# Another order of the key copies, the experts' loads and the experts' sums in a transformer block with two attentions and routed experts

## The chip, the cores and the metric

The kernel runs on one core of a Trainium2 chip. The time is the device time of one execution in microseconds; of several executions the median is given.

## The reference

The input is 32 sequences of 256 tokens of 128 numbers, all float32. With `xn = layernorm(x)` the output is `x + attention(xn) + ffn(xn)`:

- `attention`: 16 heads of 8 numbers; the keys attended to are the 256 tokens of the same sequence. A score is the covariance of a query and a key plus the product of their variances, over 8. Softmax over keys, sum of values, projection by Wo.
- `ffn`: a second block over the same tokens, in which the roles of sequence and batch are exchanged. Layernorm, a causal attention over the 32 "sequences" at one token place, projection, residual `x1`; then a second layernorm, a router over 8 experts, and for each token the two best experts: `gelu(h w1[e]) w2[e]`, weighted by the router's gate, summed and added to `x1`.

```
probs = softmax(cov(q, k) / D + var(q) var(k) / D)
x1 = xn + causal_attention(layernorm(xn)) @ out_proj
hn2 = layernorm(x1)
gates, top2 = top_k(softmax(hn2 @ router_w.T), 2)
out = x + probs @ v @ Wo + x1 + sum over top2 of gate * gelu(hn2 @ w1[e]) @ w2[e]
```

## The kernel before

The order in which each engine works is written out by hand: the instructions of an engine run in the order of the program's lines, and engines wait for each other by semaphores only.

**Causal attention** (`first_rounds`, `last_rounds`, L450 to L538). 16 chunks of 512 tokens go through layernorm, projections, scores, weights and the router's logits. `resd` in device memory gets `x + x1` (L427), `zx` in SBUF keeps the normalised tokens for the experts, `lg` the logits.

**The other attention** (`step`, L926). 32 sequences with two groups of eight heads give NU = 64 units. A unit has eight heads and is walked through in four steps, t = 8u + 0, 2, 4, 6, called x = 0, 2, 4, 6 below; each step first does two heads of scores in two senses (`scores_of`, L597): `sm`, query against key, LEAD = 14 heads ahead, for the maximum over keys (VectorE, L625); and `sT`, key against query, for the exponentials (ScalarE, L628). The maximum is turned and added to the queries "qa" two units later (L674), so that the exponentials need no more subtraction. Around these, by x:

- x = 0: in odd units `turn` (transposes of a finished sequence, L682, copied at L684), in even ones `close` (projection L690, added to the residual at L691); then `weigh_head` for the last unit's second half (pav, L637).
- x = 2: `project` and `project_rest` for a sequence two ahead (L560, ScalarE's sq L566 and qk L568, VectorE's L577 and L579).
- x = 4: `divide_lessen` (transposes L656, L659, division L664, L667, the maximum's addition L674), `turn_qk` for unit u + 3 (transposes L587 into a PSUM bank "pqk", and three copies out of it: qa by ScalarE L592, the keys "ka" in two halves, each masked for one of two heads, by VectorE L594 and ScalarE L595), and in even units `gather` (GpSimd, L551: copies one sequence's tokens out of `xnT` into "xs", two buffers) and `fetch_residual` (SyncE, L555).
- x = 6: `weigh_head` for this unit's first half.

PSUM has eight banks: four go round among sT, pav, pt, px and pe (`bank_u`), four among sm, pp, pqk, po, py and ph (`bank_w`). A new tile waits until every reader of the fourth last one is done.

**Routing** (`route`, L720) is a generator. `some(n)` (L919) lets it go n items on before each step: in units 0 to 11 four items a unit, which are VectorE's small operations over all tokens; from unit 12 on eight a unit, which are GpSimd's 128 indirect DMAs (L804) that scatter rows of `zx` to their place in `xsd`, sorted by expert.

**Experts** (`experts`, L864). At t = 256, the start of unit 32, 71 blocks of 256 rows are done in one go. `fetch` (L824) loads a block's rows from `xsd` by a DMA on GpSimd's queue, four blocks ahead; `select` (L828) reads the block's expert into a VectorE register and copies its weights; `enter` (L834) transposes the rows and scales them (L840); `hidden` (L844) is the first layer with Gelu (L850); `leave` (L852) the second layer, the copy "ye" (L861) and the store to `ysd`, also on GpSimd's queue (L862).

**Sums** (`combine`, L887), a second generator, is then drawn on by five items a unit. For each sequence, four indirect DMAs on GpSimd's queue gather its tokens' two expert rows (L894); two sequences later GpSimd multiplies by the gates (L907) and adds twice to the residual (L909). If the residual isn't loaded yet, an item does nothing. `part` (L881) stores a sequence (SyncE, L885) once both `close` and the sums have been added.

Of the kernel before, what the change touches and what calls it, by code (L numbers as in the profile page):

```python
# [11 lines left out]
F32 = mybir.dt.float32  # L12
BF16 = mybir.dt.bfloat16
I32 = mybir.dt.int32
AF = mybir.ActivationFunctionType
# [4 lines left out]
P = 128  # L20
NB = 32
SEQ = 256
NH, HD = 16, 8
NE, FF = 8, 256
NCHUNK = 16
NTILE = 64
BLK = 256
NBLK = 2 * NTILE * P // BLK + NE - 1
# [40 lines left out]
def block_kernel(  # L69
# [21 lines left out]
    nc = tc.nc  # L91
# [9 lines left out]
    half = cst[:, C_HALF:C_HALF + 2]  # L101
# [11 lines left out]
    xsd = dp.tile([NBLK * BLK, P], F32, name="xsd")  # L113
# [37 lines left out]
    def bank_u(shape, name):  # L151
        return pu.tile(shape, F32, tag="u", name=name)

    def bank_w(shape, name):
        return pw.tile(shape, F32, tag="w", name=name)
# [389 lines left out]
    NU = 2 * NB  # L545
# [7 lines left out]
    def fetch_residual(s):  # L553
        res[s] = b2.tile([P, 2, P], F32, tag="res", name=f"res{s}", bufs=NB // 2 + 4)
        nc.sync.dma_start(res[s], resd[s].rearrange("(i t) e -> t i e", t=P))  # L555
# [25 lines left out]
    def turn_qk(u):  # L581

        s, g = divmod(u, 2)
        pp = bank_w([P, 2, 2, P], f"pqk{u}")
        for n in range(2):
            for ti in range(2):
                nc.tensor.transpose(  # L587
                    pp[:, n, ti, :], qkts[s % NQ][:, ti, n, g].rearrange("p m r -> p (m r)"), ident
                )
        pp = pp.rearrange("p n t m -> p n (t m)")  # L590
        qas[u] = qa = bh.tile([P, SEQ], F32, tag="qa", name=f"qa{u}", bufs=4)
        nc.scalar.copy(qa, pp[:, 0, :])  # L592
        kas[u] = ka = bh.tile([P, 2, SEQ], F32, tag="ka", name=f"ka{u}", bufs=4)
        nc.vector.tensor_scalar(ka[:, 0, :], pp[:, 1, :], half[:, 0:1], None, ALU.mult)  # L594
        nc.scalar.activation(ka[:, 1, :], pp[:, 1, :], AF.Identity, scale=half[:, 1:2])  # L595

    def scores_of(t):  # L597

# [31 lines left out]
    def weigh_head(u, h):  # L630

        s, g = divmod(u, 2)
        if h == 0:
            pos[u] = bank_u([P, SEQ], f"pav{u}")
        for ti in range(2):
            for j in range(4):
                nc.tensor.matmul(  # L637
                    pos[u][32 * j:32 * j + 32, :],
                    vaugs[s % NV][:, ti, 4 * j + 2 * g + h, :],
                    exs[8 * u + 4 * h + j][:, ti, :],  # L640
                    start=(h == 0 and ti == 0),
                    stop=(h == 1 and ti == 1),
                )
        if h == 1:
            oas[u] = b2.tile([P, SEQ], F32, tag="oa", name=f"oa{u}")
            nc.scalar.copy(oas[u], pos.pop(u))
# [31 lines left out]
    def turn(s):  # L678
        pt = bank_w([P, 2, P], f"po{s}")
        o = ot.pop(s)  # L680
        for si in range(2):
            nc.tensor.transpose(pt[:, si, :], o[:, si, :], ident)  # L682
        oT = b2.tile([P, SEQ], F32, tag="oT", name=f"boT{s}")
        nc.vector.tensor_copy(oT, pt.rearrange("p i s -> p (i s)"))  # L684
        return oT

    def close(s, oT):
        py = bank_w([P, 2, P], f"py{s}")
        for i in range(2):
            nc.tensor.matmul(py[:, i, :], oT[:, i * P:(i + 1) * P], wo, start=True, stop=True)  # L690
        nc.vector.tensor_tensor(res[s], res[s], py, ALU.add)  # L691
        part(s)
# [120 lines left out]
    xb, wb, hb, yb = {}, {}, {}, {}  # L813
# [8 lines left out]
        gt["wall"] = wall  # L822

    def fetch(n):  # L824
        xb[n] = c2.tile([P, 2, P], F32, tag="xb", name=f"xb{n}", bufs=5)
        nc.gpsimd.dma_start(xb[n], xsd[n * BLK:(n + 1) * BLK].rearrange("(p j) w -> p j w", j=2))  # L826

    def select(n):  # L828
        e = nc.vector.value_load(gt["ebi"][0:1, n, :], min_val=0, max_val=NE - 1)
        w = c2.tile([P, 2, FF], F32, tag="w", name=f"w{n}", bufs=3)  # L830
        nc.vector.tensor_copy(w, gt["wall"][:, bass.ds(e, 1)].rearrange("p o t f -> p (o t) f"))
        wb[n] = w[:, 0, :], w[:, 1, :].rearrange("p (f h) -> p f h", f=2)

    def enter(n):  # L834
        px = bank_u([P, 2, P], f"px{n}")
        for j in range(2):
            nc.tensor.transpose(px[:, j, :], xb[n][:, j, :], ident)  # L837
        del xb[n]
        hb[n] = c2.tile([P, BLK], F32, tag="xT", name=f"xT{n}")
        nc.scalar.activation(  # L840
            hb[n], px.rearrange("p j t -> p (j t)"), AF.Identity, bias=l2b, scale=l2w
        )
# [18 lines left out]
        nc.vector.tensor_copy(ye, pe)  # L861
        nc.gpsimd.dma_start(ysd[n * BLK:(n + 1) * BLK].rearrange("(p j) h -> p j h", j=2), ye)  # L862

    def experts():  # L864
        for n in range(4):
            fetch(n)
        for n in range(-2, NBLK):
            if n >= 0 and n + 4 < NBLK:
                fetch(n + 4)
            if n + 2 < NBLK:  # L870
                select(n + 2)
                enter(n + 2)
            if 0 <= n + 1 < NBLK:
                hidden(n + 1)
            if n >= 0:
                leave(n)
# [9 lines left out]

    def combine():  # L887

        for s in range(NB + BEHIND):
            if s < NB:  # L890
                yg[s] = b2.tile([P, 2, 2, P], F32, tag="yg", name=f"yg{s}", bufs=BEHIND + 1)
                for ti in range(2):
                    for n in range(2):
                        yield nc.gpsimd.indirect_dma_start(  # L894
                            yg[s][:, ti, n, :],
                            None,
                            ysd,
                            bass.IndirectOffsetOnAxis(ap=gt["posb"][:, s, ti, n:n + 1], axis=0),
                        )
            if s >= BEHIND:  # L900
                z = s - BEHIND
                while z not in res:
                    yield True
                y = yg.pop(z)
                yf = y.rearrange("p i n e -> p (i n) e")
                gf = gt["gateb"][:, z].rearrange("p i n -> p (i n)").unsqueeze(2).to_broadcast([P, 4, P])
                nc.gpsimd.tensor_tensor(yf, yf, gf, ALU.mult)  # L907
                for n in range(2):
                    nc.gpsimd.tensor_tensor(res[z], res[z], y[:, :, n, :], ALU.add)  # L909
                part(z)  # L910

    BEHIND = 2


    LEAD = 14
    oTb = {}
    todo = []

    def some(n):  # L919
        while n > 0 and todo:  # L920
            if next(todo[0], None) is None:
                todo.pop(0)
            else:
                n -= 1

    def step(t):  # L926
        u, x = divmod(t, 8)
        scores_of(t)
        if x == 0:
            if u % 2 == 1 and 0 <= (u - 3) // 2 < NB:  # L930
                oTb[(u - 3) // 2] = turn((u - 3) // 2)
            if u % 2 == 0 and 0 <= (u - 4) // 2 < NB:
                close((u - 4) // 2, oTb.pop((u - 4) // 2))
            if 0 <= u - 1 < NU:
                weigh_head(u - 1, 1)
        if x == 2:
            if 1 <= u // 2 + 2 < NB:
                project(u // 2 + 2, u % 2)
            if 1 <= u // 2 + 2 < NB:
                project_rest(u // 2 + 2, u % 2)  # L940
        if x == 4:
            if 0 <= u - 1 < NU or 0 <= u + 1 < NU:
                divide_lessen(u - 1)
            if 1 <= u + 3 < NU:
                turn_qk(u + 3)
            if u % 2 == 0 and 2 <= u // 2 + 3 < NB:
                gather(u // 2 + 3)
            if u % 2 == 0 and 0 <= u // 2 < NB:
                fetch_residual(u // 2)
        if x == 6 and 0 <= u < NU:  # L950
            weigh_head(u, 0)

    with tc.manual_schedule():
        first_rounds()
        rest = last_rounds()
        for t in range(-LEAD, 0, 2):
            next(rest, None)
            step(t)
        assert next(rest, 0) == 0
        apools.close()  # L960
        axs.close()
        r1 = ctx.enter_context(tc.tile_pool(name="r1", bufs=1))
        b2 = ctx.enter_context(tc.tile_pool(name="b2", bufs=2))
        rts = ExitStack()
        rt = rts.enter_context(tc.tile_pool(name="rt", bufs=1))
        todo.append(route())
        for t in range(0, 8 * NU + 20, 2):
            u, x = divmod(t, 8)
            if u == NU // 2 and x == 0:
                some(1000)  # L970
                rts.close()
                c2 = ctx.enter_context(tc.tile_pool(name="c2", bufs=2))
                experts()
                todo.append(combine())
            if u < NU // 2:
                some((2, 1, 1, 0)[x // 2] if t < 96 else (3, 3, 2, 0)[x // 2])
            else:
                some((1, 1, 1, 2)[x // 2])
            step(t)
        some(1000)  # L980
# [24 lines left out]
```

## Time and profile before

| what | us |
|---|---|
| median of three runs | 1046.18 |
| lowest, highest | 1043.95, 1047.35 |
| the profiled execution itself | 1231.96 |
| its span, first to last instruction | 1230.2 |
| first "sm" (L613) starts at | 268.6 |
| first and last scatter of rows (L804) | 394.3, 670.7 |
| first "px" (L837), last "ye" (L861) of the experts | 729.5, 885.0 |
| last sum (L909) starts at | 1213.1 |
| mean granted TensorE clock | 0.919 |

A line of a group or of the timeline names the line of the program, the engine, the operation, and `out<-in` by the program's names. In the timeline the first two columns are start and duration in us; brackets give the idle time of the engine before it and what ended it. PEld is TensorE's load of weights, PE the matmuls that follow; a float32 matmul shows as two. In the list of waits the three numbers are the total in us, how often, and the longest. The profiled execution is slower than the timed ones, and the prediction has to settle first in what stretches.

### The profile page before, as it was taken

What the parts mean: (1) busy time and instruction counts of PE and PEld (TensorE: products, weight loads), DVE (VectorE), ACT (ScalarE), POOL (GpSimd) and SP (SyncE); (2) the same over time, 40 slices, a digit from 0 to 9 for tenths busy, and PEclk for the clock granted to TensorE, in tenths of its full rate; (3) what the DMA queues carried; (4) which work ended last, traced back from release to release, by engine and by line L of the source; (5) the groups of instructions that cost most, each with busy time, mean ns of one, the idle gap of its engine ahead of it and who ended that gap; (6) DMA issues with size and microseconds to landing.
All of it is one profiled execution on the core that took longest, in us unless ns stands there. A gap on an engine that the chain in (4) does not pass through costs nothing.

```text
span 1230.2 us, 32487 instructions
## 1 busy us (share of the span) xinstructions
PE 1087.6 (88%) x13107; PEld 722.8 (59%) x13107; DVE 715.9 (58%) x1702; ACT 660.0 (54%) x1298; POOL 619.1 (50%) x828
## 2 busy tenths in 40 slices
PE   4889899889999678877778999998979999999998
PEld 2667677666666244433334569888845555555564
DVE  2576777668988244443335764333447666666673
ACT  4877778734566133432234665555535555555564
POOL 6478878540001653334553015555477787775710
PEclk9998999987999688777788999999989999999999
DMA  4344443203000420000110014334311121111100
GB/s 93 124 133 132 137 137 86 68 20 103 2 1 9 51 80 26 26 24 33 35 35 21 1 32 129 121 112 126 97 51 52 53 59 49 52 53 38 42 19 19
DMA packets 80935, 76.35 MB, mean 62 GB/s; under 512 B 32841, under 2 KB 61777, under 8 KB 80785
## 3 DMA queue, kind: packets, MB, share of 16 engines
q1 hardware_dynamic: 64512, 38.72, 11.5%
q0 software_dynamic: 15008, 35.41, 9.6%
q8 instruction: 104, 1.70, 0.6%
q10 hardware_dynamic: 1264, 0.14, 0.2%
q14 instruction: 47, 0.38, 0.1%
HBM read 33.98 MB, written 40.24 MB: 60 GB/s over the span
## 4 chain that ended last, share of the span: by engine, by line
PE 67%; DVE 8%; another core or an unknown queue 7%; issue 7%; POOL 4%; ACT 3%; DMA 2%; SPq 1%; ACTq 0%; DVEq 0%; POOLq 0%
PE sm L613 20%; PE pav L637 10%; PE sT L619 8%; PE pp L560 5%; PE pe L857 3%; PE ph L848 2%; PE pqk L587 2%; PE pt L656 2%; DVE mt L625 2%; PE ptp L300 2%; PE py L690 1%; ACT ex L628 1%; DVE pr L371 1%; POOL xb L826 1%
## 5 line engine op out<-in xcount | busy, mean ns | idle before, releaser
L625 DVE TENSOR_REDUCE mt<-sm 128x2 f32<-128x512 f32 x512 | 330.9, 686 | 232.8 <-PE sT L619 77.7
L628 ACT ACTIVATE ex<-sT 128x512 f32<-128x512 f32 x512 | 279.4, 595 | 277.3 <-remote 101.9
L613 PE MATMUL sm<-ka,qa 32*128 32x256 f32 x2048 | 359.4, 431 | 30.1 <-DVE mt L625 21.3
L619 PE MATMUL sT<-qa,ka 32*128 32x256 f32 x2048 | 353.9, 427 | 28.0 <-ACT ex L628 16.6
L613 PEld LDWEIGHTS sm<-ka,qa 32*128 32x128 f32 x2048 | 206.1, 196 | 154.0 <-DVE mt L625 67.1
L619 PEld LDWEIGHTS sT<-qa,ka 32*128 32x128 f32 x2048 | 208.8, 196 | 56.3 <-ACT ex L628 32.6
L637 PE MATMUL pav<-ex,va 128*32 128x256 f32 x2048 | 165.7, 390 | 26.6 <-issue 24.5
L804 POOL DMA_INDIRECT xsd<-zx,posi x128 | 123.5, 965 | 53.1 <-issue 37.5
L894 POOL DMA_INDIRECT yg<-ysd,posb x128 | 122.9, 960 | 38.4 <-issue 29.6
L551 POOL COPY xs<-xnT 128x256 f32<-128x256 f32 x32 | 20.0, 626 | 217.1 <-PE pp L560 210.0
L637 PEld LDWEIGHTS pav<-ex,va 128*32 128x32 f32 x2048 | 58.6, 109 | 101.9 <-issue 76.1
L862 POOL DMA_DIRECT2D ysd<-ye x71 | 45.3, 638 | 94.8 <-DVE ye L861 91.4
L857 PEld LDWEIGHTS pe<-w,ge 128*128 128x128 f32 x568 | 74.4, 191 | 4.2 <-ACT ge L850 0.6
L909 POOL TENSOR_TENSOR res<-res,yg 128x256 f32<-128x256 f32 x64 | 46.6, 728 | 57.8 <-DMA res<-resd 28.5
L857 PE MATMUL pe<-w,ge 128*128 128x128 f32 x568 | 74.9, 275 | 0.2 <-ACT ge L850 0.2
L848 PE MATMUL ph<-xT,w 128*128 128x256 f32 x284 | 73.4, 381 | 0.5 <-ACT xT L840 0.5
L595 ACT ACTIVATE ka<-pqk,cst 128x256 f32<-128x256 f32 x64 | 30.4, 474 | 73.5 <-DVE ka L594 67.1
L861 DVE COPY ye<-pe 128x256 f32<-128x256 f32 x71 | 30.2, 425 | 66.3 <-PE pe L857 66.3
L560 PE MATMUL pp<-wqkv,xs 128*128 128x384 f32 x128 | 66.9, 609 | 0.0
L840 ACT ACTIVATE xT<-px,vec 128x256 f32<-128x256 f32 x71 | 40.0, 565 | 47.8 <-PE px L837 47.8
L370 DVE TENSOR_REDUCE mx<-sc 128x16 f32<-128x512 f32 x64 | 43.4, 678 | 19.9 <-PE sc L355 19.9
L850 ACT ACTIVATE ge<-ph 128x512 f32<-128x512 f32 x71 | 42.4, 597 | 21.9 <-PE ph L848 21.9
(171 smaller groups left out, 1717.8 us busy)
## 6 DMA issues: line engine op xcount, KB each, us to landing
xb<-xsd POOLq DMA_DIRECT2D x71, 128.0 KB
ysd<-ye POOLq DMA_DIRECT2D x71, 128.0 KB
xsd<-zero SPq DMA_DIRECT2D x10, 852.0 KB
vald<-v SPq DMA_DIRECT2D x16, 288.0 KB
vb<-vald SPq DMA_DIRECT2D x64, 72.0 KB
xt<-in_L_attn_x_dram SPq DMA_DIRECT2D x64, 64.0 KB
resd<-xt SPq DMA_DIRECT2D x64, 64.0 KB
res<-resd SPq DMA_DIRECT2D x32, 128.0 KB
```

Of the source, the lines that this page charges most:

```text
L560: nc.tensor.matmul(pp.rearrange("p n m -> p (n m)"), xs[s][:, ti * P:(ti + 1) * P], wqkv.rearrange("p n m -> p (n m)"), start=True, stop=True,
L613: nc.tensor.matmul(sc[:, i, :], qas[u][r:r + 32, i * P:(i + 1) * P], kas[u][r:r + 32, h, :], start=True, stop=True,)
L619: nc.tensor.matmul(sc[:, i, :], kas[u][r:r + 32, h, i * P:(i + 1) * P], qas[u][r:r + 32, :], start=True, stop=True,)
L625: nc.vector.tensor_reduce(mts[y // 8 % 2][:, :, o:o + 1], sc, AX.X, ALU.max, negate=True)
L628: nc.scalar.activation(exs[y], sc, AF.Exp, scale=1.0 / HD)
L637: nc.tensor.matmul(pos[u][32 * j:32 * j + 32, :], vaugs[s % NV][:, ti, 4 * j + 2 * g + h, :], exs[8 * u + 4 * h + j][:, ti, :], start=(h = ...
L804: yield nc.gpsimd.indirect_dma_start(xsd_views[n * NTILE + k], bass.IndirectOffsetOnAxis(ap=posi[:, k, n:n + 1], axis=0), zx[:, k, :], None,)
L848: nc.tensor.matmul(ph[:, f, :], wb[n][0][:, f * P:(f + 1) * P], xT, start=True, stop=True)
L857: nc.tensor.matmul(pe[:, j, :], ge[:, f, j * P:(j + 1) * P], w2b[:, f, :], start=(f == 0), stop=(f == 1))
L862: nc.gpsimd.dma_start(ysd[n * BLK:(n + 1) * BLK].rearrange("(p j) h -> p j h", j=2), ye)
L894: yield nc.gpsimd.indirect_dma_start(yg[s][:, ti, n, :], None, ysd, bass.IndirectOffsetOnAxis(ap=gt["posb"][:, s, ti, n:n + 1], axis=0),)
L909: nc.gpsimd.tensor_tensor(res[z], res[z], y[:, :, n, :], ALU.add)
```

## The change

- `turn_qk`: ScalarE's half of "ka" stands ahead of VectorE's half, right behind the copy of the queries.
- `fetch`: the experts' rows are loaded by SyncE in place of GpSimd, six blocks ahead in place of four, in seven buffers in place of five; the selected weights have four buffers in place of three.
- The entry: the pool of the experts' tiles is opened, six blocks are fetched and two experts selected at t = 252 (half a unit earlier); the x = 0 work of unit 32 (`close`, `weigh_head`) is issued inside the experts, between the second block's transposes and the first block's first layer.
- `combine` takes the sequences in the order 0 to 23, 28 to 31, 24 to 27; the residuals of sequences 23 to 30 are loaded two at a time in units 46 to 52, that of 31 in unit 54.

```diff
@@ turn_qk
         kas[u] = ka = bh.tile([P, 2, SEQ], F32, tag="ka", name=f"ka{u}", bufs=4)
+        nc.scalar.activation(ka[:, 1, :], pp[:, 1, :], AF.Identity, scale=half[:, 1:2])
         nc.vector.tensor_scalar(ka[:, 0, :], pp[:, 1, :], half[:, 0:1], None, ALU.mult)
-        nc.scalar.activation(ka[:, 1, :], pp[:, 1, :], AF.Identity, scale=half[:, 1:2])
@@ fetch, select
-        xb[n] = c2.tile([P, 2, P], F32, tag="xb", name=f"xb{n}", bufs=5)
-        nc.gpsimd.dma_start(xb[n], xsd[n * BLK:(n + 1) * BLK].rearrange("(p j) w -> p j w", j=2))
+        xb[n] = c2.tile([P, 2, P], F32, tag="xb", name=f"xb{n}", bufs=AHEAD + 1)
+        nc.sync.dma_start(xb[n], xsd[n * BLK:(n + 1) * BLK].rearrange("(p j) w -> p j w", j=2))
...
-        w = c2.tile([P, 2, FF], F32, tag="w", name=f"w{n}", bufs=3)
+        w = c2.tile([P, 2, FF], F32, tag="w", name=f"w{n}", bufs=4)
@@ experts
-    def experts():
-        for n in range(4):
+    AHEAD = 6
+    def enter_experts():
+        for n in range(AHEAD):
             fetch(n)
+        for n in range(2):
+            select(n)
+    def experts(between):
         for n in range(-2, NBLK):
-            if n >= 0 and n + 4 < NBLK:
-                fetch(n + 4)
+            if n >= 0 and n + AHEAD < NBLK:
+                fetch(n + AHEAD)
             if n + 2 < NBLK:
-                select(n + 2)
+                if n >= 0:
+                    select(n + 2)
                 enter(n + 2)
+            if n == -1:
+                between()
@@ combine
-        for s in range(NB + BEHIND):
-            if s < NB:
+        order = [*range(NB - 8), *range(NB - 4, NB), *range(NB - 8, NB - 4)]
+        for i in range(NB + BEHIND):
+            if i < NB:
+                s = order[i]
...
-            if s >= BEHIND:
-                z = s - BEHIND
+            if i >= BEHIND:
+                z = order[i - BEHIND]
...
+    RESIDUALS = {NB - 9 + i: [NB - 9 + 2 * i, NB - 8 + 2 * i] for i in range(4)} | {NB - 5: [NB - 1]}
@@ step
-        if x == 0:
-            (the x = 0 work)
+        if x == 0 and u != NU // 2:
+            first_quarter(u)
...
-                fetch_residual(u // 2)
+                for s in RESIDUALS.get(u // 2, [u // 2] if u // 2 < NB - 9 else []):
+                    fetch_residual(s)
@@ the main loop
-            if u == NU // 2 and x == 0:
+            if t == 4 * NU - 4:
                 some(1000)
                 rts.close()
                 c2 = ctx.enter_context(tc.tile_pool(name="c2", bufs=2))
-                experts()
+                enter_experts()
+            if t == 4 * NU:
+                experts(lambda: first_quarter(u))
                 todo.append(combine())
```

`first_quarter(u)` is the x = 0 work of `step`, taken out as a function of its own without a change.

More of the change, by code (lines that the diff above doesn't have):

```diff
@@ L924, in some, with first_quarter @@
                 n -= 1
+    def first_quarter(u):
+        if u % 2 == 1 and 0 <= (u - 3) // 2 < NB:
+            oTb[(u - 3) // 2] = turn((u - 3) // 2)
+        if u % 2 == 0 and 0 <= (u - 4) // 2 < NB:
+            close((u - 4) // 2, oTb.pop((u - 4) // 2))
+        if 0 <= u - 1 < NU:
+            weigh_head(u - 1, 1)
     def step(t):
@@ L928, in step @@
         scores_of(t)
-        if x == 0:
[L930 to L935, printed above, removed]
+        if x == 0 and u != NU // 2:
+            first_quarter(u)
         if x == 2:
```

## The prediction

> **What bounds the kernel now.** I read the page first (span, busy shares, chain), then stretches of 20 us, then one undisturbed unit of the timeline, then the waits, then GpSimd's timeline in the second half.
>
> ```profile
> span 1230.2 us, 32487 instructions
> PE 1087.6 (88%) x13107; PEld 722.8 (59%) x13107; DVE 715.9 (58%) x1702; ACT 660.0 (54%) x1298; POOL 619.1 (50%) x828
> ...
> PE 67%; DVE 8%; another core or an unknown queue 7%; issue 7%; POOL 4%; ACT 3%; DMA 2%; SPq 1%; ACTq 0%; DVEq 0%; POOLq 0%
> ```
>
> TensorE carries 67% of the chain, so a wait counts only if TensorE stands in it. But this execution took 1231.96 us (its span and 1.76 around it), 186 more than the median of 1046.18, and where the surplus lies decides what may be read from it. The stretches tell (columns: PE, PEld, DVE, ACT, POOL busy, granted clock, DMA):
>
> ```profile
> 340.00:360.00 20.00, 20.00 (x232) 12.73 (x229) 16.48 (x40) 12.27 (x27) 1.89 (x4) 1.00 0.00 1
> 480.00:500.00 20.00, 11.73 (x69) 5.03 (x65) 3.27 (x6) 2.86 (x5) 13.50 (x15) 0.82 0.15 50
> ```
>
> While GpSimd issues a row of sixteen indirect DMAs (480 to 500) TensorE starts its matmuls late, for no wait that the profile shows. One copy "qa" (L592) starts per unit: its starts lie 9.27 and 9.54 apart by turns from 681 to 728, where nothing disturbs (mean 9.40), 27 to 31 every other unit from 402 to 681, and 10.9 on average after the experts. Sixteen units from 389.7 to 681.2 take 291.5, at 9.40 they would take 150.4: 141 too much. 28 units from 892.3 to 1196.5 take 304.2 for 263.2: 41 too much. 1232 less 182 is 1050, 0.4% over the median. So I take the surplus for the profiled execution's own, take 9.40 us as a unit of the timed runs, and subtract savings from 1046.2.
>
> Inside an undisturbed unit:
>
> ```profile
> 708.75 0.38 ACT L592 COPY qa<-pqk 128x256 f32<-128x256 f32 x1
> ...
> 709.93 0.48 DVE L594 TENSOR_SCALAR ka<-pqk,cst 128x256 f32<-128x256 f32 x1
> ...
> 710.44 0.47 ACT L595 ACTIVATE ka<-pqk,cst 128x256 f32<-128x256 f32 x1 [1.31 <-DVE ka L594]
> 710.72 0.43 PEld L613 LDWEIGHTS sm<-ka,qa 32*128 32x128 f32 x3 [0.41 <-DVE ka L594]
> ...
> 710.82 1.08 ACT L628 ACTIVATE ex<-sT 128x512 f32<-128x512 f32 x2
> ...
> 711.46 0.18 PEld L619 LDWEIGHTS sT<-qa,ka 32*128 32x128 f32 x1 [0.19 <-ACT ex L628]
> ...
> 712.51 0.52 PEld L690 LDWEIGHTS py<-wo,boT 128*128 128x128 f32 x4 [0.33 <-issue]
> ...
> 714.15 0.19 PEld L613 LDWEIGHTS sm<-ka,qa 32*128 32x128 f32 x2 [0.41 <-DVE res L691]
> ...
> 715.23 0.30 PEld L560 LDWEIGHTS pp<-wqkv,xs 128*128 128x128 f32 x2 [0.33 <-issue]
> ```
>
> ScalarE stands 1.31 us behind its half of "ka" until VectorE's half is done; the two exponentials queued behind it start at 710.82, though their scores were written by about 709.9. TensorE's next step of scores needs a PSUM bank of the first of them: its fourth matmul loads at 711.46, 0.74 after the step began. The step takes 710.72 to 712.51, 1.79; the next, without such a wait, 714.15 to 715.23, 1.08. This stands in every unit with a turned key.
>
> **What the Trainium skill says.** "PSUM — Partial Sum Buffer", section "PSUM bank collisions raise a hardware error": two engines may not use one bank and quadrant at once, reads included, so their accesses are ordered by semaphores. The trace agrees: ka's halves, both read from pqk's bank, never overlap. "DMA: Bandwidth & Descriptors", section "SWDGE vs HWDGE vs iDMA": descriptors of GpSimd's DMAs are built by software, those of SyncE by hardware, free of VectorE's lock on GpSimd's port. The waits below show GpSimd held once for 3.4 us by "w". "TensorE: Matmul & The Clock Gate", section "HAM oscillation — how this bites in real kernels": idle gaps of TensorE over some 3.4 us lower its clock. Stretches of 4 us agree: 1.00 at 448, 0.50 from 456 to 468, after gaps.
>
> **1. Key copies.** Both halves stay; only the order turns. ScalarE does qa and its half in a row (done at about 709.6); VectorE's half waits for it, but VectorE is busy with den, ot and qa until 709.93 anyway, so that the wait costs nothing; behind it stand the two maxima at 710.33, unmoved (cover 0.3 us; gone, each 0.1 late costs 0.1 a unit). The exponentials start at 709.9, the first ends at 710.5, before TensorE asks at 710.72. The bank of pqk is now let go by VectorE's half at 710.41, also before. So the step falls from 1.79 to 1.08: 0.71 a unit, 9.40 to 8.69. Next in line is VectorE: its maxima end at 711.61, the next scores come at 711.9; 0.3 spare.
> Where it counts:
> - units 0 to 11: VectorE also does the routing (16.5 to 19.4 of each 20 us busy), and about half is left: 0.35 x 12 = 4 (bounds 0 and 8.5).
> - units 12 to 31: 0.71 x 20 = 14.2. But GpSimd has to scatter 8 rows a unit at 1.265 us (0.96 and 0.30 between), and every second unit a gather (0.5 more): 10.37 a unit, while TensorE now needs 8.69. The gather is queued 1.75 units ahead of its use, and scatters start 9 us before TensorE's unit 12 (394.3 against about 403). At the last gather under scatters GpSimd is at -9 + 14 x 10.37 + 10.7 (8 scatters and the gather itself) = 146.9, TensorE wants it at 16 x 8.69 + 3.8 (from a unit's start to its L560, 884.85 to 888.64) = 142.8: 4 given back, 10 left. (Before: 154.2 against 146.9, no wait.)
> - units 32 to 60: 0.71 x 29 = 20.6, against part 4.
>
> **2. Experts' rows by SyncE, seven buffers for five, fetched six ahead.**
>
> ```profile
> PE px L837 <- DMA xb<-xsd: 8.7, 7, 2.3
> PEld px L837 <- DVE w L831: 7.5, 4, 2.4
> POOL ysd L862 <- DVE w L831: 3.4, 1, 3.4
> ```
>
> xT (L840) starts 2.012 us apart as a mean, but for a few gaps of 2.3 to 4.4: 147.1 us over 68 blocks against 68 x 2.012 = 136.8, 10.3 in gaps. Those are late rows: a fetch stands in GpSimd's queue behind the store of "ye", which waits for the block's end. On SyncE nothing is ahead of it but fetches; a load issues in 0.37 to 0.46 there, 71 of them in 2.01 each. All gaps go: 10 (bounds 6 and 10.3). Four buffers of w for three cover VectorE's copies; GpSimd's stores lose their neighbour and can't be later. SyncE's only later work is the residual of unit 32, due three units on.
>
> **3. Entry prepared.** Between the first transpose (729.53) and the first second-layer matmul (733.57) TensorE has 0.75 + 1.74 of work in 4.04 us: 1.5 idle. The change puts the projection and pav of unit 32's first quarter there (0.64 + 1.0), and two select copies (2 x 0.43) go earlier, into unit 31's slack of VectorE. ScalarE's copy of pav now stands ahead of the first Gelu with its 1.28 table load, some 0.4 late: saves 1.2 (0 to 2).
>
> **4. Sums in another order.** The number of gathers and adds stays; residuals 24 to 31 come earlier, so the sums no longer wait for them near the end (two waits of 14 us on GpSimd in the profile, hidden: TensorE was at work till the end). What counts is the pace:
>
> ```profile
> 921.31 0.94 POOL L894 DMA_INDIRECT yg<-ysd,posb  x1 [0.30 <-issue]
> 922.27 1.05 POOL L907 TENSOR_TENSOR yg<-yg,gateb 128x512 f32<-128x512 f32 x1
> 923.41 1.53 POOL L909 TENSOR_TENSOR res<-res,yg 128x256 f32<-128x256 f32 x2
> 925.21 0.98 POOL L894 DMA_INDIRECT yg<-ysd,posb  x1 [0.27 <-POOL res L909]
> ```
>
> A sequence costs GpSimd 7.69 us (941.04 to 948.72 is one whole), 1.25 of them a unit, and 0.26 for gathers: 9.87 a unit against TensorE's 8.69. First gather done 8.1 after TensorE's start at 884.85, the one of k units later at 8.1 + 9.87k; TensorE wants it at 3.8 + 8.69 (k + 2). From k = 12 GpSimd is late, at the last gather (k = 24) by 15.2. So part 1 keeps 20.6 - 15.2 = 5.4 here. With the old order the sums would have paused from k = 21, which would have saved about 3.5 of this. Behind late sums SyncE's residual loads wait too, 2.5 units at most of the 3.5 that they have: free.
>
> **Sum.** 4 + 10 + 10 + 1.2 + 5.4 = 30.6: 1046.2 - 30.6 = 1015.6, say 1015.
>
> **Rivals.**
> - GpSimd's issue is not so dear without the profiler, or its slack is larger: then 4 and 15.2 are not given back, 996. For: the surplus shows that profiling weighs on just these stretches. Against: 0.96 and 0.30 are the same beside an idle TensorE. 18%.
> - Another wait takes the place of the one removed (VectorE's maxima with 0.3 spare, or the scores' banks): part 1 gives a third of its 38.8, 13, of which GpSimd takes back about 1: 1046 - 12 - 11 = 1023; with none, 1035. Middle 1030. For: VectorE's thin cover. Against: 1.2 us that VectorE idles before other maxima. 20%.
> - Slower: the late gathers make TensorE wait some 2.4 us every second unit, and its clock falls as at 456 to 468, 12 us at half, 6 lost each time. At ten waits (seven late pairs in the second half, three in the first) 60 lost: 1075. From five drops on the gain is gone. For: the clock did fall after gaps. Against: 2.4 is less than the gaps there, and a slow TensorE lets GpSimd catch up. 7%.
> - The change does nothing that counts, because the timed runs are bound by GpSimd already and the gaps of the experts are the profiler's: 1046. 5%.
>
> **How the numbers follow.** The forecast has 50%, alone 1006 to 1024. 0.3% (3.1 us) is about what a measurement of this kernel can tell from no change. Faster: 50 + 18 + 20 = 88%; same 5; slower 7. The range leaves out the slow rival, the null and the ends of the others: 993 to 1037.
>
> **What would show it.** Right: in undisturbed units qa's starts 8.7 apart, ScalarE's "ka" without wait, the step of scores 1.1 long; no xT interval over 2.3 and some 143 us from first px to the last ye (before 155); after the experts L560 waiting for xs. Wrong if undisturbed units stay over 9.1, or if VectorE's "ka" waits and delays its maxima, or if the time falls under 1000 (GpSimd then sets no pace).

## The result, and the profile after

| | us |
|---|---|
| before, median of 4 runs | 1045.07 (1043.12 to 1047.35) |
| after, median of 4 runs | 1035.14 (1034.08 to 1035.70) |
| ratio | 0.9903, 95% interval 0.9878 to 0.9928 |
| the profiled execution of after | 1034.63, span 1032.8 |
| forecast | 1015, range 993 to 1037 |

The change makes the kernel 1.0% faster, 10 us, where 31 were forecast. On four of the six chips used for the experiments, and in the profile of before, the kernel before takes 1.17 to 1.20 times as long as here (the last section shows where that time goes), so times are compared within a set of runs on one chip, and where two sets are compared the text says so.

The page of after, the same parts as shown of before: the span, TensorE's busy time, and the engines' shares of the chain that ended last.

```profile
span 1032.8 us, 32436 instructions
PE 953.5 (92%) x13107; PEld 665.8 (64%) x13107; DVE 710.4 (69%) x1702; ACT 654.7 (63%) x1298; POOL 582.3 (56%) x757
...
PE 70%; POOL 12%; DVE 8%; issue 5%; ACT 3%; DMA 1%; SPq 0%; DVEq 0%; POOLq 0%; ACTq 0%
```

GpSimd (POOL) has risen from 4% to 12% of the chain. The stretches tell where (PE, PEld, DVE, ACT, POOL busy, clock, DMA):

```profile
340.00:360.00 20.00, 20.00 (x242) 12.21 (x241) 17.73 (x41) 12.41 (x28) 1.90 (x4) 1.00 0.01 2
480.00:500.00 20.00, 20.00 (x263) 11.90 (x255) 16.66 (x38) 13.15 (x29) 15.43 (x17) 1.00 0.16 52
960.00:980.00 20.00, 5.16 (x59) 3.04 (x55) 3.10 (x6) 3.09 (x7) 15.92 (x19) 0.66 0.15 44
```

From 480 to 500 GpSimd scatters rows and TensorE works without a pause; the surplus that the profile of before had there is missing. From 960 to 980 TensorE works a quarter of the time, while GpSimd is as busy as ever.

A unit of after, for the one that the prediction showed of before:

```profile
337.53 0.38 ACT L592 COPY qa<-pqk 128x256 f32<-128x256 f32 x1
...
337.78 0.50 ACT L594 ACTIVATE ka<-pqk,cst 128x256 f32<-128x256 f32 x1
...
338.70 0.47 DVE L595 TENSOR_SCALAR ka<-pqk,cst 128x256 f32<-128x256 f32 x1
338.71 1.08 ACT L628 ACTIVATE ex<-sT 128x512 f32<-128x512 f32 x2 [0.43 <-PE sT L619]
339.49 0.19 PEld L613 LDWEIGHTS sm<-ka,qa 32*128 32x128 f32 x2 [0.41 <-DVE ka L595]
...
340.57 0.52 PEld L690 LDWEIGHTS py<-wo,boT 128*128 128x128 f32 x4 [0.33 <-DVE mt L625]
```

ScalarE's half of "ka" follows "qa" without a wait, the exponentials wait for scores and no longer for VectorE, and the step of scores lasts from 339.49 to 340.57, 1.08 for 1.79 before. Undisturbed units start 8.55 and 8.82 apart by turns, 8.69 as a mean, which is the forecast to the last digit.

The list of waits of after (total, times, longest). No wait of "px" for the rows "xb" or for "w" is left in it; these have come in:

```profile
DVE res L691 <- POOL res L923: 16.6, 1, 16.6
...
PE sm L613 <- DVE res L691: 14.8, 1, 14.8
PE pp L560 <- POOL xs L551: 13.6, 5, 3.3
```

The last line is the late gathers, which were forecast. The two ahead of it are one stall, which was not: TensorE stands 14.8 us for VectorE's addition of a projection into a residual (`close`, L691), which stands 16.6 us for GpSimd's sums in the same residual (L923). The chain of after there (start, us, what):

```profile
972.64 0.07 POOL res L923
...
973.32 1.05 POOL yg L921
...
977.80 0.77 POOLq L1022
...
978.59 0.43 DVE res L691
...
979.07 1.39 PE sm L613 x3
...
980.48 0.41 PE sm L613 x2
...
984.30 0.20 PE sm L613 x2
```

GpSimd works its queue off to the very end (the piece at 977.80 is the last), only then VectorE adds, and only then TensorE goes on. When TensorE stopped, at about 964.2, GpSimd still had some 14 us of queued work. Two matmuls of "sm" then take 0.41 till about 984, and 0.20 after that. "TensorE: Matmul & The Clock Gate", section "HAM oscillation — how this bites in real kernels", of the Trainium skill says that an idle gap of some 3.4 us puts TensorE on half clock; the trace agrees, with a granted clock of 0.50 from 968 to 983 and of 1.00 from 984. The unit lasts 26.14 us: 17.5 over 8.69, of which 14.8 are the wait and the rest mostly the half clock (TensorE works at it from 979.07 to about 983.5).

Why just there: `close(27)` stands in unit 58, and the new order puts the sums of 27 last. They are handed out in unit 57, right ahead of it, in one go with those of 25 and 26. TensorE waits for the addition itself: of the four banks that go round, the first scores of the second step after `close` take the one that holds the projection "py", which the addition has to read first. They start at 979.07, when the addition (978.59, 0.42 long) is done. VectorE's queue is in order, so the maxima behind the addition are late as well.

### The profile page after: what moved, and what is told of

It reads as the page before. It is cut to its first block, busy times and chain, and to the rows that moved or that the text cites. A ratio compares the mean times of both kernels' runs of the same rounds, so it can differ in the third digit from the quotient of the medians.

```text
span 1032.8 us, 32436 instructions
## 1 busy us (share of the span) xinstructions
PE 953.5 (92%) x13107; PEld 665.8 (64%) x13107; DVE 710.4 (69%) x1702; ACT 654.7 (63%) x1298; POOL 582.3 (56%) x757
## 4 chain that ended last, share of the span: by engine, by line
PE 70%; POOL 12%; DVE 8%; issue 5%; ACT 3%; DMA 1%; SPq 0%; DVEq 0%; POOLq 0%; ACTq 0%
PE sm L613 21%; PE pav L637 10%; PE pe L857 6%; PE ph L848 6%; POOL xsd L804 5%; PE pp L560 5%; POOL yg L908 2%; PE pqk L587 2%; PE sT L619 2%; PE ptp L300 2%; PE pt L656 2%; DVE pr L371 2%; DVE mx L370 1%; PE px L837 1%; PE py L690 1%
## 5 line engine op out<-in xcount | busy, mean ns | idle before, releaser
L613 PE MATMUL sm<-ka,qa 32*128 32x256 f32 x2048 | 300.9, 407 | 18.2 <-DVE res L691 14.8
L619 PE MATMUL sT<-qa,ka 32*128 32x256 f32 x2048 | 293.7, 405 | 0.1
L613 PEld LDWEIGHTS sm<-ka,qa 32*128 32x128 f32 x2048 | 183.8, 187 | 122.1 <-DVE mt L625 53.1
L619 PEld LDWEIGHTS sT<-qa,ka 32*128 32x128 f32 x2048 | 178.1, 186 | 2.6 <-issue 1.2
L637 PE MATMUL pav<-ex,va 128*32 128x256 f32 x2048 | 137.0, 385 | 0.0
L637 PEld LDWEIGHTS pav<-ex,va 128*32 128x32 f32 x2048 | 53.4, 109 | 52.8 <-ACT ka L594 16.3
L560 PE MATMUL pp<-wqkv,xs 128*128 128x384 f32 x128 | 61.0, 559 | 14.5 <-POOL xs L551 13.6
L374 ACT ACTIVATE pr<-pr 128x1024 f32<-128x1024 f32 x32 | 33.8, 1057 | 35.6 <-DVE pr L371 35.6
L831 DVE COPY w<-wall 128x512 f32 x71 | 30.3, 427 | 32.2 <-issue 30.9
L848 PEld LDWEIGHTS ph<-xT,w 128*128 128x128 f32 x284 | 48.4, 190 | 4.0 <-ACT xT L840 0.4
```

Source lines behind the costliest of these rows:

```text
L560: nc.tensor.matmul(pp.rearrange("p n m -> p (n m)"), xs[s][:, ti * P:(ti + 1) * P], wqkv.rearrange("p n m -> p (n m)"), start=True, stop=True,
L613: nc.tensor.matmul(sc[:, i, :], qas[u][r:r + 32, i * P:(i + 1) * P], kas[u][r:r + 32, h, :], start=True, stop=True,)
L619: nc.tensor.matmul(sc[:, i, :], kas[u][r:r + 32, h, i * P:(i + 1) * P], qas[u][r:r + 32, :], start=True, stop=True,)
L637: nc.tensor.matmul(pos[u][32 * j:32 * j + 32, :], vaugs[s % NV][:, ti, 4 * j + 2 * g + h, :], exs[8 * u + 4 * h + j][:, ti, :], start=(h = ...
L848: nc.tensor.matmul(ph[:, f, :], wb[n][0][:, f * P:(f + 1) * P], xT, start=True, stop=True)
```

## The experiments

Theory A, formed on these traces: parts 1 to 3 do about what the forecast said, and part 4, counted as free, costs the 17.5 us of the wait for the sums of 27. Rival B: GpSimd is simply late by so much, and without this wait TensorE would stand at another place.

### First set: on a chip where nothing is late

The kernel before, without an edit, one profiled execution.

> The kernel before, unchanged, for a second profile. If the surplus of 186 us (27 to 31 us units beside rows of indirect DMAs) came from that one profiled execution, this span lies at 1042 to 1050, units at 9.4 throughout, and no gather is late. If profiling this kernel always costs it, the span is again near 1230. If undisturbed units are shorter than 9.4 and the rest is waits for GpSimd, then the price of 1050 was right only by chance: the span is near 1045, with waits of L560 for xs or of L691 for sums of several us.

Measured: 1226.8 us. The three others were timed beside it, where the kernel before takes 1233.7 us (median of 7). First, the exchange of the key copies alone:

```diff
+        nc.scalar.activation(ka[:, 1, :], pp[:, 1, :], AF.Identity, scale=half[:, 1:2])
         nc.vector.tensor_scalar(ka[:, 0, :], pp[:, 1, :], half[:, 0:1], None, ALU.mult)
-        nc.scalar.activation(ka[:, 1, :], pp[:, 1, :], AF.Identity, scale=half[:, 1:2])
```

> Part 1 alone on the kernel before. Theory (sums late): units at 8.69, gathers late by 4 in the first half and 4 in the second, and the projection of sequence 26 (unit 56) waits some 12 us for GpSimd's sums, which are queued just ahead of it: 1045 - 39 + 8 + 12 = 1026 (1020 to 1031). Rival (the keys' saving isn't in the timed runs): 1040 or more. Rival (no cost of late sums outside the new order): 1014.

Measured: ratio 0.9899 (0.9857 to 0.9940).

The changed kernel with 27 taken ahead of 28 to 31, and then with the old order and the old times of the residuals:

```diff
-        order = [*range(NB - 8), *range(NB - 4, NB), *range(NB - 8, NB - 4)]
+        order = [*range(NB - 8), *range(NB - 5, NB), *range(NB - 8, NB - 5)]
```

> The changed kernel, with sequence 27 summed ahead of 28 to 31 (its sum is then queued five units ahead of its projection, and 24 to 26 after theirs). Theory (VectorE's addition of sequence 27's projection waits for all that is queued on GpSimd, TensorE behind it): the wait of 16.6 us at L691 goes, the late gathers stay, 1035 - 17 = 1018 (1015 to 1022). Rival (the amount of GpSimd's work binds, whatever the order): the wait turns up elsewhere, 1032 to 1036.

Measured: ratio 0.9787 (0.9747 to 0.9826).

```diff
-        order = [*range(NB - 8), *range(NB - 4, NB), *range(NB - 8, NB - 4)]
+        order = [*range(NB)]
...
-    RESIDUALS = {NB - 9 + i: [NB - 9 + 2 * i, NB - 8 + 2 * i] for i in range(4)} | {NB - 5: [NB - 1]}
+    RESIDUALS = {s: [s] for s in range(NB)}
```

> The changed kernel with the sums and the residuals in the order of the kernel before (parts 1 to 3 stay). Theory: some close still crosses the late sums (sequence 26, unit 56), but at a smaller lag, some 12 us for 20: 1035 - 8 = 1027 (1022 to 1031). Rival (the new order is what makes the sums block): no wait of L691, 1016. Rival (the new order gains): above 1037.

Measured: ratio 0.9807 (0.9758 to 0.9856). The three edited kernels missed their times in us, which had been set for a chip with 1045; the unedited one came out near the 1230 of its second case, but not because profiling always costs it: the profiled executions of the second set are free of it. TensorE is slowed beside the rows of indirect DMAs here, so that GpSimd isn't behind (none of these traces has a wait of L691 for GpSimd's sums, or of L560 for "xs"), and the two orders can't be told apart. The set says nothing on A and B, but it says that the surplus of 186 us is not that one profiled execution's own: all runs of the kernel before here, at 1226.8 to 1236.8 us, have it too.

### Second set: on a chip like that of the result

The kernel before takes 1049.3 us here (median of 29, 1042.7 to 1056.5). The changed kernel as it is:

> The changed kernel as it is, as the yardstick of this set of runs. Both theories expect the ratio to the kernel before that was measured, 0.99, where the kernel before takes 1045 us. If the chip of this set is one of those on which the kernel before takes about 1230 us, GpSimd is no longer late there, so the 17 us wait for the sums of sequence 27 should be missing and the ratio should be near that of the order with 27 first, 0.98.

Measured: 1034.9 us, ratio 0.9851 (0.9794 to 0.9908), and the unit of 26.15 us is in its trace again.

The order with 27 first, as above:

> The changed kernel with one edit: the sums of sequence 27 stand ahead of 28 to 31, so that VectorE's addition into its residual is due long after GpSimd's. Theory A (the 17 us wait of VectorE for GpSimd's sums of 27 is what the forecast missed): 17 us less than the changed kernel, 1018 us where that takes 1035; the longest unit becomes 14 to 15 us and no wait of VectorE for GpSimd's sums is left. Rival B (GpSimd is simply late by that much, and the wait moves to a gather or to the end): 1030 to 1035 us. Where the kernel before takes 1230 us: no difference from the changed kernel.

Measured: 1017.0 us (1016.1 to 1019.9), ratio 0.9684 (0.9629 to 0.9739). That is 17.9 us less than the changed kernel for one number in one line. In its list of waits that of L691 for GpSimd is gone, while TensorE's waits for the late gathers stand as they were:

```profile
PE pp L560 <- POOL xs L551: 13.6, 5, 3.3
```

B is out: GpSimd is as late as before (the waits for the late gathers are the same 13.6 us), and TensorE doesn't stand at another place for it.

Part 4 alone, on the kernel before (the hunks of `combine` and of `fetch_residual` in the diff of the change, and no other):

> The kernel before with the new order of sums and residuals alone. Theory A: GpSimd is late there too, by less since a unit takes 9.4 us; counting its queue gives a wait of 9 us for the sums of 27, so 1054 us where the kernel before takes 1045 (ratio 1.009). Rival (the order is free by itself, and turns bad only with the shorter units): 1045 us, no difference. Where the kernel before takes 1230 us: no difference.

Measured: 1060.4 us (1056.3 to 1062.0), ratio 1.0107 (1.0082 to 1.0132), 11 us slower. Its trace, of the fastest of its twelve executions, has one unit of 19.10 us among units of 9.26 and 9.54, and these waits:

```profile
DVE res L691 <- POOL res L911: 9.3, 1, 9.3
PE sm L613 <- DVE res L691: 7.1, 1, 7.1
```

So the new order isn't free by itself: it costs 9.7 us (19.10 less 9.40) in long units, and 17.5 in short ones, in which GpSimd falls further behind.

Parts 2 and 3 alone (the changed kernel with the key copies, the order of sums and the residuals of the kernel before):

> The changed kernel with the key copies and the order of sums of the kernel before: experts' rows by SyncE, four weight buffers and the prepared entry alone. The forecast's terms are 10 us for the blocks and 1.2 us for the entry: 1034 us where the kernel before takes 1045 (ratio 0.989). Rival (the rows were only part of the stall, and something of it comes back in the sums just after): 1040 us, ratio 0.995. Where the kernel before takes 1230 us the saving in us should be about the same, ratio 0.99.

Measured: 1045.1 us (1038.8 to 1047.5), ratio 0.9941 (0.9922 to 0.9959): 6.2 us, nearer to the rival's 0.995. The trace shows 8.9 us saved over the experts (153.24 from the last "qa" ahead of them to the first after, 162.16 with part 4 alone), and then a last stretch 5 us longer than with part 4 alone, at a clock of 0.80 and 0.73. The traced execution is the slowest of the 18, and one execution doesn't tell whether that stretch belongs to the kernel, so some 3 us stay open. It also has a unit of 11.22 us with this wait:

```profile
DVE res L691 <- POOL res L923: 3.2, 1, 3.2
```

So with the old order too an addition already waited for the sums, in long units, in this kernel.

### Third and fourth set, and two more runs: the late gathers

Two edits of the kernel with 27 first. Gathers two sequences further ahead, with two more buffers:

```diff
-        xs[s] = bh.tile([P, SEQ], F32, tag="xs", name=f"xs{s}", bufs=2)
+        xs[s] = (b2 if s > 3 and s % 4 > 1 else bh).tile([P, SEQ], F32, tag="xs", name=f"xs{s}", bufs=2)
...
+    GATHERS = {-1: [2], 0: [3], 1: [4], 2: [5, 6], 3: [7, 8]}
...
-            if u % 2 == 0 and 2 <= u // 2 + 3 < NB:
-                gather(u // 2 + 3)
+            if u % 2 == 0:
+                for s in GATHERS.get(u // 2, [u // 2 + 5] if 4 <= u // 2 < NB - 5 else []):
+                    gather(s)
```

and sums handed out more slowly, `some((1, 1, 1, 1)[x // 2])` for `some((1, 1, 1, 2)[x // 2])`. With them ran the kernel before and the key copies alone.

> The kernel before as it is, one look, for a profile of an execution of about 1045 us. Theory A: units of 9.26 and 9.54 us throughout, no unit of 27 to 31 us beside the rows of indirect DMAs, and one wait of VectorE for GpSimd's sums of at most 3 us, as in the kernel with the experts' part alone. Rival (the stalls beside indirect DMAs are part of this kernel): units of 20 to 30 us there, and 1230 us.

> The kernel before with the key copies exchanged, and nothing else. The forecast: 4 + 10 + 5.4 = 19.4 us less, 1026 us where the kernel before takes 1045. Theory A adds a wait of VectorE for GpSimd's sums of sequence 26 in the old order, 12 us by counting the queues, with the late gathers before it making up for part: 1028 to 1038 us, with that wait in the trace. Rival (the old order of sums has no such wait): 1024 to 1026 us.

> The order with 27 first, and gathers two sequences further ahead (four buffers for them in place of two). Theory A (the units of 13 to 14.5 us are late gathers and cost what they are longer than 8.7 us, 20 us in all): 20 us less than the order with 27 first alone, 997 us where that takes 1017. Rival (TensorE, freed of these waits, is throttled or waits for GpSimd at the next place, its additions): 1005 to 1012 us.

> The order with 27 first, and the sums handed out in steps of 1, 1, 1, 1 per unit in place of 1, 1, 1, 2, buffers as they were. Theory A (GpSimd falls behind because it is handed five pieces of 1.3 us and a share of the sums in 8.7 us): with four it keeps up, so the three late gathers of the second half go, 15 us, 1002 us where the order with 27 first takes 1017; the one in the first half (13.7 us) stays. Rival (the last sums come so late that the end waits for GpSimd): 1010 to 1020 us.

This set fell on a chip where the kernel before takes 1231.8 us (the profiled execution 1231.2). Ratios: key copies 0.9886 (0.9860 to 0.9911), further ahead 0.9816 (0.9793 to 0.9839), slower sums 0.9821 (0.9781 to 0.9862). Run again, the same four fell on another such chip, where the kernel before takes 1248.8 us:

> The kernel before with the key copies exchanged, and nothing else, where the kernel before takes 1045 us. The forecast: 4 + 10 + 5.4 = 19.4 us less, 1026 us. Theory A adds a wait of VectorE for GpSimd's sums of sequence 26 in the old order, 12 us by counting the queues, with less late gathers after it: 1028 to 1038 us, with that wait in the trace. Rival (the old order of sums has no such wait): 1024 to 1026 us.

> The order with 27 first, and gathers two sequences further ahead (four buffers for them in place of two). Theory A (the units of 13 to 14.5 us are late gathers and cost what they are longer than 8.7 us, 20 us in all): 997 us where the order with 27 first alone takes 1017 and the kernel before 1045, ratio 0.954. Rival (TensorE, freed of these waits, is throttled or waits for GpSimd at the next place, its additions): 1005 to 1012 us, ratio 0.962 to 0.968.

> The order with 27 first, and the sums handed out in steps of 1, 1, 1, 1 per unit in place of 1, 1, 1, 2, buffers as they were. Theory A (GpSimd falls behind because it is handed five pieces in 8.7 us): with four it keeps up, so the three late gathers of the second half go, 15 us, 1002 us where the order with 27 first takes 1017, ratio 0.959; the late gather of the first half (13.7 us) stays. Rival (the last sums come so late that the end waits for GpSimd): 1010 to 1020 us.

> The kernel before as it is, one look, for a profile of an execution of about 1045 us. Theory A: units of 9.26 and 9.54 us throughout, no units of 27 to 31 us, and one wait of VectorE for GpSimd's sums of at most 3 us. Rival: such units are part of this kernel, and only the timed runs are without them.

Ratios, in the same order: 0.9865 (0.9804 to 0.9927), 0.9755 (0.9690 to 0.9821), 0.9825 (0.9761 to 0.9889); the profiled execution of the kernel before 1245.4 us. As in the first set GpSimd is hardly behind on these chips (the longest wait for it of this kind is 0.9 us), so these ratios don't tell what making it less late is worth. The slower sums were never run where they could count, and stay open. The gathers, in a run of their own, met a chip on which the kernel before takes 1049.1 us:

> The order with 27 first, and gathers two sequences further ahead (four buffers for them in place of two). Theory A (the units of 13 to 14.5 us are late gathers and cost what they are longer than 8.7 us, 20 us in all): 997 us where the order with 27 first alone takes 1017 and the kernel before 1045 to 1049, ratio 0.95. Rival (TensorE, freed of these waits, is throttled or waits for GpSimd at the next place, its additions): 1005 to 1012 us, ratio 0.958 to 0.965. Where the kernel before takes 1230 us or more: a ratio of 0.976 to 0.982 again, which tells nothing on this.

Measured: 999.3 us (998.3 to 999.5), ratio 0.9516 (0.9463 to 0.9569), and 2.3 us over A's figure; the rival's 0.958 is outside the interval. The order with 27 first took 17.7 us more in the second set; that is a comparison of two chips, on which the kernel before takes 1049.1 and 1049.3 us. In its waits this is what is left of the late gathers, and a stretch near the end, in columns as above, runs without a pause:

```profile
PEld pp L560 <- POOL xs L551: 0.7, 2, 0.3
```

```profile
940.00:960.00 20.00, 20.00 (x261) 12.14 (x254) 16.65 (x37) 13.42 (x30) 16.57 (x19) 1.00 0.16 39
```

Every unit between the experts and the last two starts 8.55 or 8.82 after the one ahead. This is the fastest version, 5% under the kernel before. The last run was meant to settle whether short units alone already bring a wait in the old order:

> The kernel before with the key copies exchanged, and nothing else, where the kernel before takes 1045 to 1049 us. The forecast: 4 + 10 + 5.4 = 19.4 us less, ratio 0.981. Theory A adds a wait of VectorE for GpSimd's sums of sequence 26 in the old order, 12 us by counting the queues, with less late gathers after it: 8 to 17 us less, ratio 0.984 to 0.992, with that wait in the trace. Rival (the old order of sums has no such wait): 19 to 22 us less, ratio 0.979 to 0.982. Where the kernel before takes 1230 us or more: ratio 0.99 again, which tells nothing on this.

Measured: ratio 0.9883 (0.9861 to 0.9906), but where the kernel before takes 1231.2 us. So it tells nothing on this. How long the old order would wait in units of 8.69 stays open, and so does what the key copies alone are worth on a chip where GpSimd is late.

## Why the prediction was wrong

The step that failed is part 4, "free". It followed GpSimd's lateness to two readers, the gathers (TensorE) and the residual loads (SyncE), and left out the third: VectorE's addition of the projection into the same residual. Whichever of the two additions stands second in the program waits for the first. By the forecast's own count GpSimd is 15.2 us late at the last gather; the sums of 27, last in the new order, are queued behind it and right ahead of `close(27)`. The term was 0 and is 17.5. The run with 27 first, which removes it alone, is 32.2 us under the kernel before of its set, where the forecast's other terms add to 30.6. That 1035 lies inside the stated range all the same is luck: neither the forecast nor a rival has this term.

The other terms, read from the traces of part 4 alone and of the changed kernel, both of the second set and both free of the surplus (starts of "qa", the two waits for sums, 9.7 and 17.5, taken out; the late gathers by pairs of units, of which an undisturbed one takes 17.37; one unit's saving of 0.71 that falls into the stretch of the experts is counted with units 32 to the end):

| term | forecast | measured |
|---|---|---|
| undisturbed unit | 9.40 to 8.69 | 9.40 to 8.69 |
| units 0 to 11 | 4 | 7.0 |
| units 12 to 31, net | 10 | 7.2 |
| the late gather in it | 4 | 6.1 (two pairs, 4.96 and 1.15) |
| experts, 71 blocks | 10 | 10.2 (147.93 to 137.77, first to last xT) |
| entry, and what else lies between the last "qa" ahead of the experts and the first after | 1.2 | -1.1 |
| units 32 to the end, net | 5.4 | 5.9 |
| the late gathers in it | 15.2 | 15.4 (4.67 + 4.71 + 6.05) |
| sum | 30.6 | 29.2 |

This is one trace of each kernel, and that of part 4 alone is 4 us under the median of its twelve executions, so the sum holds to a few us.

- The base was right, for a wrong reason. The surplus was taken for "the profiled execution's own"; runs of the kernel before take 1231 to 1249 us on such chips, profiled or not. That it lay outside the timed runs of 1046 was true, and so was the unit of 9.40 without it.
- Units 0 to 11: VectorE's routing hides less than the half taken. Units 12 to 31: the gather came 6.1 late for 4. The two errors cancel, which is luck.
- The debt to the gathers was the finest part: counted 15.2, measured 15.4, though in three steps where the forecast has TensorE late at seven gathers. The list of waits gives TensorE only 13.6 for all five; the units are 21.5 longer. Beside each of the four waits of 3.0 to 3.3 us the clock is down (in the trace of after 0.79 from 540 to 548 and from 860 to 868, 0.66 from 904 to 909, 0.57 from 942 to 950).
- The entry has two halves. From the first transpose to the first second-layer matmul it now takes 4.50 us with 1.64 of moved work in it, 2.86 for 4.04: 1.2 saved, as forecast. In the traces of parts 2 and 3 alone and of the gathers further ahead, with the same entry, it takes 5.02 and 5.55, so the saving isn't firm. And the two copies of weights that go early were to fit "into unit 31's slack of VectorE". They don't, as the timeline of after shows:

```profile
572.92 0.43 DVE L831 COPY w<-wall 128x512 f32 x1 [1.21 <-ACT ex L628]
573.71 0.43 DVE L831 COPY w<-wall 128x512 f32 x1 [0.36 <-issue]
574.05 1.28 DVE L625 TENSOR_REDUCE mt<-sm 128x2 f32<-128x512 f32 x2
...
574.79 0.48 PE L613 MATMUL sm<-ka,qa 32*128 32x256 f32 x1 [1.75 <-DVE mt L625]
```

The copies stand ahead of two maxima, with 1.21 and 0.36 us before them in which VectorE also reads the block's expert into a register, 2.4 in all. TensorE waits 1.75 for the first maximum, more than the entry saves; 1.2 less 1.75 is -0.6, of the -1.1 measured. The rest is open.

- The experts' rows by SyncE and the fourth weight buffer together gave the 10 of the forecast; no run separates them. What the prediction says of VectorE's lock on GpSimd's port no run here shows: the wait of 3.4 us that it names stands behind a copy of VectorE (L831) by semaphore.
- Of the rivals, "slower" rested on the clock falling after late gathers. It does fall, but all that the late gathers cost beyond the waits themselves is some 8 us (21.5 less 13.6), not 60. Nor do the stretches that it cites agree with a limit of 3.4 us: in the profile of before the clock is 1.00 from 448 to 452, 0.90 from 452 to 456 and 0.50 after that, and from 448 to 456 TensorE never stands longer than 1.70 (the lines are in the last section). The rival at 1030, "another wait takes the place of the one removed", is near in time by luck: part 1 gave all its 0.71 a unit, and the wait is another than it named.

## What to carry to other kernels

An in-place sum that two engines add to makes whichever stands second in the program wait for the other: when one engine's queue is known to be late, look up every later instruction of other engines that touches the same tile, and give the tiles that are touched soonest to the late engine first. Look also at what waits for that instruction: here it held a PSUM bank. A late queue was made harmless here by distance and not by speed: the kernel with 27 first and gathers further ahead does the same work on GpSimd and is 3.4% faster than the changed one (0.9516 over 0.9851, each against the kernel before on its own chip). Whether handing the sums out more slowly does it too was not shown. A step moved early, "into slack", is checked against the instruction that stands behind it in its new place, register reads included.

## What the runs showed of the hardware

Where the kernel before takes 1231 us, the time goes in stretches beside GpSimd's rows of indirect DMAs. In the profile of before (start, duration, idle time in brackets; then a stretch in columns as above):

```profile
448.51 0.64 PE L637 MATMUL pav<-ex,va 128*32 128x256 f32 x4 [0.33 <-issue]
...
449.93 0.65 PE L637 MATMUL pav<-ex,va 128*32 128x256 f32 x4 [0.79 <-issue]
...
451.37 0.65 PE L637 MATMUL pav<-ex,va 128*32 128x256 f32 x4 [0.78 <-issue]
...
452.80 0.59 PE L637 MATMUL pav<-ex,va 128*32 128x256 f32 x2 [0.78 <-issue]
...
455.71 0.79 PE L613 MATMUL sm<-ka,qa 32*128 32x256 f32 x1 [1.70 <-DVE mt L625]
```

```profile
448.00:452.00 4.00, 2.10 (x13) 0.48 (x12) 0.00 (x0) 0.00 (x0) 3.09 (x4) 1.00 0.18 63
```

TensorE gets some four matmuls off every 1.42 us and stands in between for nothing that the profile shows (only the last line waits for VectorE). The clock is not what slows it first: it is still 1.00 from 448 to 452, and falls to 0.50 only after that. Every second unit under scatters takes 27 to 33 us for 9.4. In the second set, with the same row of sixteen scatters in the same place (480 to 500), TensorE is busy 20.00 of 20 us, where the profile of before has 11.73. The duration of an indirect DMA on GpSimd is the same in both, 0.96. It was so in every run on four chips and in none on two; what differs between them isn't known.
